# Layer 2 of a four-layer graph network: the low part of the messages made by VectorE straight from PSUM instead of from a second ScalarE copy

## The chip, the core and the metric

The kernel runs on one core of one Trainium2 chip. The metric is the device time of one launch in microseconds (us), taken as the median of three runs: 2426.45 us before the change (2425.6 to 2430.18). The profile is one further execution; its own time is 2429.41 us, and its span, from the first to the last instruction, is 2428.0 us.

## What is computed

Sixteen graphs of 1024 nodes with 256 features go through four layers; each layer is x = x + gnn(relu(layernorm(x))) (layer 3 the same with a four-headed attention). The change is in layer 2:

```python
h = jnp.maximum(_layernorm(x, axis=-1), 0.0)
a = adj.astype(x.dtype)
h2 = jnp.einsum('bnf,fu->bnu', h, W_msg)            # messages
msg_sum = jnp.einsum('bij,biu->bju', a, h2)         # summed over the neighbours i
deg = jnp.sum(a, axis=1)
messages = jnp.where(deg[..., None] > 0, msg_sum / jnp.maximum(deg, 1.0)[..., None], 0.0)
x = x + relu(jnp.einsum('bnf,fu->bnu', h, W_upd) + messages + bias)
```

## The kernel before

**Tiles.** A graph's 1024 nodes are eight tiles of 128 rows (NT = 8), its 256 features two chunks of 128 (DC = 2). `xs` holds a graph's x; `ht` is the normalised, transposed x that feeds the projections. The transposes (`flip`, line 930, by TensorE into `pt_h`) and the copies into `ht` (line 931, ScalarE) are made four at a time.

**Layer 2, first part: projections (lines 1153 to 1160).** For each of the eight node tiles n, `project` (line 936) multiplies `ht` by W_msg into a PSUM tile `ps_proj`. It is full float32, so each of its two matmuls is two passes of TensorE: four matmul instructions in the trace for one n. All projections of all layers share the two buffers of the pool `mm_ps` (tag "mm"); the projection two places later needs the buffer back. The message is then split in two parts that TensorE can multiply in its faster one-pass form F32R: ScalarE writes `hi` = ps_proj times z, rounded to F32R (line 1156), writes the same product again, unrounded, into a float32 tile `rest` in SBUF (line 1158; two buffers, tag "e", which other layers' `e` tiles share), and VectorE writes `lo` = `rest` minus `hi` (line 1159). So `ps_proj` is free again when ScalarE has done line 1158.

**Layer 2, second part: neighbour sums (lines 1161 to 1182).** For each of eight output tiles j, into one PSUM bank `ps_o2` (two buffers): two chunks of the W_upd product (line 1164), then eight F32R matmuls with `hi` and eight with `lo` (line 1170), whose stationary operand is the adjacency `adj_n[j]`, brought in by GpSimd's DMA queue (line 828). ScalarE takes the result out (lines 1178, 1179), VectorE adds the bias and the residual (lines 1180, 1006).

**The order.** Nothing runs in the order in which it is written. Graphs are laid out some 130 us apart in a list of due times, so that the layers of one graph stand beside layers of the next, and then the class `Order` plays the whole program against a table of costs per instruction and writes a fixed order for each engine. At each moment it gives an engine the ready instruction that is earliest in the list. A changed instruction can therefore move its neighbours on every engine. Once built, each engine's queue is strictly in order: an instruction that waits holds up all that stand behind it.

**Beside the projections of layer 2** in the same stretch stand the last projections of layer 0 of the next graph (line 936 with 258 columns, copied out by ScalarE, line 1022), and the last transposes of layer 2's own input, whose scales VectorE makes (lines 901, 902) and ScalarE applies (line 911, `hn`). Lines 986 and 991 are two short VectorE instructions of layer 0, line 953 and the DMAs 955 and 961 make layer 0's row of weights. Layer 3 (line 1225 on VectorE, line 1238 on TensorE with 64-column halves), layer 1 (lines 1109 and 1102) and layer 0 (lines 1048, 1050, 1040) are not touched.

Of the kernel before, what the change touches and what calls it, by code (L numbers as in the profile page):

```python
# [9 lines left out]
F32 = mybir.dt.float32  # L10
U8 = mybir.dt.uint8
AF = mybir.ActivationFunctionType
OP = mybir.AluOpType
AX = mybir.AxisListType

P = 128
# [630 lines left out]
def tile_simple_stack(  # L647
# [11 lines left out]
    nc = tc.nc  # L659
    B, N, D = x.shape  # L660
# [23 lines left out]
    def tile_of(pool, shape, dtype, tag, name, bufs):  # L684
        t = pool.tile(shape, dtype, tag=tag, name=name, bufs=bufs)
        slots[t.tensor.tag] = bufs
        return t
# [11 lines left out]
    work = ctx.enter_context(tc.tile_pool(name="work", bufs=2))  # L699
# [123 lines left out]
    def load_adj(b, g):  # L823

        t = tile_of(state, [P, NT, EIGHTH], F32R, tag="adj", name="adj", bufs=4)
        if b == 0 and g < 4:
            behind(t[:1, 0, :1])
        nc.gpsimd.dma_start(t, adj[b, :, g * EIGHTH : (g + 1) * EIGHTH].rearrange("(i p) c -> p i c", p=P))  # L828
        return t
# [103 lines left out]
    def project(norm, w, n, width):  # L933
        ps = tile_of(mm_ps, [P, HALF], F32, tag="mm", name="ps_proj", bufs=2)
        for c in range(DC):
            nc.tensor.matmul(ps[:, :width], norm.ht[:, c, n * P : (n + 1) * P], w[:, c, :width], start=(c == 0), stop=(c == DC - 1))  # L936
        return ps
# [58 lines left out]
    def residual(xs, i, v, after, e=None):  # L996

        x = xs[:, i, :]
        if i % 2 == 0:
            if i == NT - 2:  # L1000
                after.settle()
            after.flip()
            after.sums = tile_of(small, [P, 2], F32, tag="sums", name="sums", bufs=4)
        if e is not None:
            nc.vector.scalar_tensor_tensor(x, e, 1.0, x, op0=OP.min, op1=OP.add)
        nc.vector.scalar_tensor_tensor(x, v, 0.0, x, op0=OP.max, op1=OP.add, accum_out=after.sums[:, i % 2 : i % 2 + 1])  # L1006
        if i % 2:
            after.pair(xs, i // 2, after.sums)
# [130 lines left out]
    def layer2(b, xs, norm, after):  # L1139

        adj_n = [load_adj(b, g) for g in range(4)]
        z = tile_of(small, [P, NT], F32, tag="z2", name="z2", bufs=2)
        nc.vector.reciprocal(z, norm.times)
        hi = tile_of(state, [P, NT, W3], F32R, tag="hs", name="hi", bufs=3)
        lo = tile_of(state, [P, NT, W3], F32R, tag="hs", name="lo", bufs=3)
        nc.vector.memset(hi[:, :, D : D + 1].bitcast(F32), 1.0)  # L1150
        nc.vector.memset(hi[:, :, D + 1 : D + 2].bitcast(F32), 0.0)
        nc.vector.memset(lo[:, :, D : D + 2].bitcast(F32), 0.0)
        for n in range(NT):
            ps = project(norm, wx[2], n, D)
            by = z[:, n : n + 1]
            nc.scalar.activation(hi[:, n, :D], ps[:, :D], AF.Copy, scale=by)  # L1156
            rest = tile_of(work, [P, D], F32, tag="e", name="rest", bufs=2)
            nc.scalar.activation(rest, ps[:, :D], AF.Copy, scale=by)
            nc.vector.tensor_tensor(lo[:, n, :D], rest, hi[:, n, :D].bitcast(F32), op=OP.subtract)
            yield 0.91  # L1160
        for j in range(NT):
            ps = tile_of(hd_ps, [P, HALF], F32, tag="hd", name="ps_o2", bufs=2)
            for c in range(DC):
                nc.tensor.matmul(  # L1164
                    ps[:, :D], norm.ht[:, c, j * P : (j + 1) * P], wx[2][:, c, D:], start=(c == 0), stop=False,
                    skip_group_check=True,
                )
            for h in (hi, lo):
                for i in range(NT):
                    nc.tensor.matmul(  # L1170
                        ps[:, : D + 2], adj_n[j][:, i, :], h[:, i, : D + 2],
                        start=False, stop=(h is lo and i == NT - 1), skip_group_check=True,
                    )
            k = b * NT + j
            if j + 4 < NE:
                adj_n.append(load_adj(b, j + 4))
            v = tile_of(work, [P, D], F32, tag="v", name="v", bufs=2)
            nc.scalar.activation(v, ps[:, :D], AF.Copy, scale=z[:, j : j + 1])
            nc.scalar.copy(edges[:, k : k + 1], ps[:, D : D + 1])
            nc.vector.tensor_tensor(v, v, rows["bias2"], op=OP.add)  # L1180
            residual(xs, j, v, after)
            yield 1.61
# [120 lines left out]
    def graph(b):  # L1303
        xs = loaded.pop(b)
        m = masks.pop(b)
        norm = Norm()
        if b == 0:
            norm.first = tile_of(small, [P, NT], F32, tag="q", name="first", bufs=4)
        for g in range(NT // 2):
            norm.pair(xs, g)  # L1310
            m.step()
            yield 2.74
        for layer, inputs in ((layer0, (m,)), (layer1, (m.bytes,)), (layer2, ())):
            yield 1.81
            norm.settle()
            norm.flip()
            after = Norm(degrees(b) if layer is layer1 else None)
            yield from layer(b, xs, *inputs, norm, after)
            norm = after
        yield 1.19  # L1320
        norm.flip()
        res = tile_of(state, [P, NT, H, HW], F32, tag="res", name="res", bufs=1)
        hs = yield from layer3(b, xs, m.bytes, norm, res)
        return tail(b, xs, hs, res)
# [51 lines left out]
    ps = tile_of(tr_ps, [P, P], F32, tag="tr", name="ps_bad", bufs=2)  # L1376
# [65 lines left out]
```

## Time and profile before

| | us |
|---|---|
| median of three runs | 2426.45 (2425.6 to 2430.18) |
| the profiled execution, its own time | 2429.41 |
| its span | 2428.0 |
| TensorE (PE) busy | 2361.5, 97% of the span |
| TensorE weight loads (PEld) busy | 2106.7 |
| VectorE (DVE) busy | 1964.4, 81% |
| ScalarE (ACT) busy | 1455.2, 60% |
| GpSimd (POOL) busy | 469.3 |
| mean granted TensorE clock | 0.991 |

A group of instructions is shown with its line, engine, operation, the tiles that it writes and reads, shapes, count, busy time, mean duration, and the idle time of its engine just before it with what ended that. A matmul's duration in the trace is longer than its share of the pipeline, since several are under way at once; so a TensorE that is "busy" can still lose time, and the time from the start of one matmul to the start of the next says more than the busy time does. The chain of work that ended last goes back from the last instruction, at each step to what released it.

The three instructions of the change are groups of 128 (16 graphs by 8 tiles): line 1156 on ScalarE, 60.1 us, 470 ns each; line 1158 on ScalarE, 59.0 us, 473 ns each; line 1159 on VectorE, 53.7 us, 425 ns each.

### The profile page before, as it was taken

The numbers are of one execution on the slowest core, as the hardware profiler recorded it, in microseconds if no ns is written. First come the engines' busy times: TensorE is split into PE (matmuls) and PEld (weight loads), VectorE is DVE, ScalarE is ACT, GpSimd is POOL, SyncE is SP. The second block draws the span as 40 slices with busy tenths as digits, with TensorE's granted clock in tenths as the row PEclk, the third lists the DMA queues.
The fourth block names the chain that finished last, engine by engine and source line by source line (L and its number), as shares of the span: only waits on it lengthen the run. The fifth ranks groups of instructions, "written<-read, shape, count | busy, mean of one in ns | idle before, by whom it ended". The sixth has DMA issues, their size and how long they took to land.

```text
span 2428.0 us, 63180 instructions
## 1 busy us (share of the span) xinstructions
PE 2361.5 (97%) x26244; PEld 2106.7 (87%) x26244; DVE 1964.4 (81%) x3871; ACT 1455.2 (60%) x4062; POOL 469.3 (19%) x454
## 2 busy tenths in 40 slices
PE   7999999999999999999999999999999999999984
PEld 5889888988888889888998989889888998989874
DVE  6478697996979888787897969879787896978867
ACT  5765657567475665757567475665757566475340
POOL 1120310303113031220303113031220303103021
PEclk9999999999999999999999999999999999999997
DMA  5452342624344263342624334263342634244021
GB/s 177 88 110 89 70 97 87 140 85 92 94 105 101 84 126 98 79 97 78 142 93 92 93 101 106 84 119 101 84 97 75 144 93 92 89 104 89 19 63 37
DMA packets 212008, 231.65 MB, mean 95 GB/s; under 512 B 10328, under 2 KB 160960, under 8 KB 211712
## 3 DMA queue, kind: packets, MB, share of 16 engines
q0 software_dynamic: 137728, 83.90, 19.5%
q1 hardware_dynamic: 73984, 143.62, 18.9%
q8 instruction: 208, 3.41, 0.6%
q14 instruction: 88, 0.72, 0.1%
HBM read 210.25 MB, written 17.22 MB: 94 GB/s over the span
## 4 chain that ended last, share of the span: by engine, by line
PE 86%; DMA 5%; ACT 4%; DVE 3%; POOL 1%; issue 1%; SPq 0%; ACTq 0%; DVEq 0%
PE ps_o L1238 18%; PE ps_o L1040 17%; PE ps_proj L936 17%; PE ps_o L1102 16%; PE ps_o L1170 10%; PE ps_o L1164 4%; PE pt_h L930 4%; DMA raw<-in_adj_t 4%; ACT mask L820 1%; DVE p L1225 1%; POOL rs L836 1%; ACT hn L911 1%; ACT hi L1156 1%; DMA d_row<-e_row 0%; DMA row<-d_row 0%
## 5 line engine op out<-in xcount | busy, mean ns | idle before, releaser
L1225 DVE SCALAR_TENSOR_TENSOR p<-row,q,mask 128x1024 f32<-128x1024 f32 x512 | 617.9, 1279 | 63.0 <-PE ps_o L1238 58.6
L936 PE MATMUL ps_proj<-wx,ht 128*128 128x258 f32 (+2 forms) x2048 | 514.3, 387 | 6.7 <-ACT hs L1194 3.9
L1238 PEld LDWEIGHTS ps_o<-hb,p 128*64 128x64 f32 x16384 | 488.1, 138 | 27.8 <-issue 20.6
L1238 PE MATMUL ps_o<-hb,p 128*64 128x65 f32 x16384 | 502.2, 223 | 4.7 <-DVE p L1225 2.3
L1040 PE MATMUL ps_o<-hs,p 128*128 128x256 f32 x2048 | 477.8, 381 | 4.3 <-ACT hs L1052 4.3
L1102 PE MATMUL ps_o<-hs,p 128*128 128x257 f32 x2048 | 468.8, 382 | 3.9 <-ACT v L1127 2.2
L1102 PEld LDWEIGHTS ps_o<-hs,p 128*128 128x128 f32 x2048 | 381.5, 190 | 61.4 <-ACT v L1127 6.9
L936 PEld LDWEIGHTS ps_proj<-wx,ht 128*128 128x128 f32 x2048 | 371.7, 191 | 67.6 <-ACT hs L1082 6.5
L1040 PEld LDWEIGHTS ps_o<-hs,p 128*128 128x128 f32 x2048 | 381.1, 191 | 54.8 <-ACT hs L1052 4.7
L835 POOL TENSOR_SCALAR rs<-mv 128x4 f32<-128x4 f32 (+1 forms) x112 | 44.9, 401 | 1317.6 <-ACT unread L884 1298.9
L836 POOL TENSOR_TENSOR rs<-rs,neg_half 128x4 f32<-128x4 f32 (+2 forms) x144 | 265.9, 1846 | 12.0
L911 ACT ACTIVATE hn<-xs,shift 128x256 f32<-128x256 f32 x384 | 177.1, 504 | 77.3 <-PE pt_h L930 43.0
L1170 PE MATMUL ps_o<-hi,adj 128*128 128x258 f32 x1024 | 202.3, 320 | 2.1 <-ACT hi L1156 1.0
L1246 ACT ACTIVATE res<-ps_o 128x260 f32<-128x260 f32 x128 | 49.8, 389 | 254.2 <-PE ps_o L1238 253.9
L820 ACT ACTIVATE mask<-raw 128x512 uint8<-128x512 int32 x248 | 156.1, 632 | 53.6 <-DMA raw<-in_adj_t 52.7
L930 PE MATMUL pt_h<-ident,hn 128*128 128x128 f32 x1024 | 175.8, 278 | 2.0 <-ACT hn L911 1.8
L1006 DVE SCALAR_TENSOR_TENSOR xs<-v,xs 128x256 f32<-128x256 f32 x384 | 160.3, 418 | 17.8 <-ACT v L1127 11.2
L828 POOL DMA_DIRECT2D adj<-in_adj x128 | 114.8, 899 | 293.9 <-PE ps_o L1170 292.3
L1170 PEld LDWEIGHTS ps_o<-hi,adj 128*128 128x128 f32 x1024 | 150.1, 190 | 14.9 <-ACT hi L1156 5.4
L1048 DVE SCALAR_TENSOR_TENSOR p<-row,q 128x1024 f32<-128x1024 f32 x128 | 161.4, 1271 | 1.8 <-ACT row L980 1.6
L930 PEld LDWEIGHTS pt_h<-ident,hn 128*128 128x128 f32 x1024 | 126.0, 141 | 36.5 <-ACT hn L911 10.3
L931 ACT COPY ht<-pt_h 128x512 f32<-128x512 f32 x256 | 147.1, 575 | 16.8 <-PE pt_h L930 14.0
(124 smaller groups left out, 3009.0 us busy)
## 6 DMA issues: line engine op xcount, KB each, us to landing
raw<-in_adj_t SPq DMA_DIRECT2D x256, 256.0 KB
adj<-in_adj POOLq DMA_DIRECT2D x128, 512.0 KB, 5.3
row<-d_row SPq DMA_DIRECT2D x108, 512.0 KB
xs<-in_x POOLq DMA_DIRECT2D x32, 512.0 KB, 4.4
out<-xs SPq DMA_DIRECT2D x32, 512.0 KB
wx<-in_w SPq DMA_DIRECT2D x3, 256.0 KB
d_row<-e_row SPq DMA_DIRECT2D x45, 4.0 KB
wts<-in_w_t SPq DMA_DIRECT2D x2, 256.0 KB
```

The lines of the kernel that those rows point to most:

```text
L820: nc.scalar.activation(to, raw, AF.Square, accum_out=total)
L836: nc.gpsimd.tensor_tensor(rs[:, :n], rs[:, :n], neg_half[:, :n], op=OP.pow)
L911: nc.scalar.activation(hn, xs[:, 2 * g + k, :], AF.Relu, scale=scale, bias=bias)
L930: nc.tensor.transpose(pt[:, c, k * P : (k + 1) * P], hn[:, c * P : (c + 1) * P], ident)
L936: nc.tensor.matmul(ps[:, :width], norm.ht[:, c, n * P : (n + 1) * P], w[:, c, :width], start=(c == 0), stop=(c == DC - 1))
L1006: nc.vector.scalar_tensor_tensor(x, v, 0.0, x, op0=OP.max, op1=OP.add, accum_out=after.sums[:, i % 2 : i % 2 + 1])
L1040: nc.tensor.matmul(ps[:, :D], ps_[j][:, i * P : (i + 1) * P], hs[:, j, :D], start=(j == 0), stop=(j == NT - 1))
L1048: nc.vector.scalar_tensor_tensor(p, row_a, q[:, j : j + 1], row_b, op0=OP.mult, op1=OP.max)
L1102: nc.tensor.matmul(ps[:, : D + 1], ps_[j][:, i * P : (i + 1) * P], hs[:, j, : D + 1], start=(j == 0), stop=(j == NT - 1))
L1170: nc.tensor.matmul(ps[:, : D + 2], adj_n[j][:, i, :], h[:, i, : D + 2], start=False, stop=(h is lo and i == NT - 1), skip_group_check=True,)
L1225: nc.vector.scalar_tensor_tensor(p, row, q[:, jj, h : h + 1], mask[:, jj, :], op0=OP.max, op1=OP.mult)
L1238: nc.tensor.matmul(pss[g][part, k * HW : (k + 1) * HW], ps_[t][:, i * P : (i + 1) * P][:, part], hbv[:, j + t, h, :], start=(j == 0 and t ...
```

## The change

One pass on VectorE takes the place of one on ScalarE and one on VectorE. `lo` is now ps_proj times z minus `hi`, read from PSUM by VectorE; the tile `rest` is gone. The buffer `ps_proj` is now free when VectorE has done this pass.

```diff
             ps = project(norm, wx[2], n, D)
             by = z[:, n : n + 1]
             nc.scalar.activation(hi[:, n, :D], ps[:, :D], AF.Copy, scale=by)
-            rest = tile_of(work, [P, D], F32, tag="e", name="rest", bufs=2)
-            nc.scalar.activation(rest, ps[:, :D], AF.Copy, scale=by)
-            nc.vector.tensor_tensor(lo[:, n, :D], rest, hi[:, n, :D].bitcast(F32), op=OP.subtract)
+            nc.vector.scalar_tensor_tensor(
+                lo[:, n, :D], ps[:, :D], by, hi[:, n, :D].bitcast(F32), op0=OP.mult, op1=OP.subtract
+            )
             yield 0.91
```

The new instruction is line 1157 of the changed kernel.

## The prediction

> **What bounds the kernel now.** I read the page first: the busy times, then the chain of work that ended last.
>
> ```profile
> PE 2361.5 (97%) x26244; PEld 2106.7 (87%) x26244; DVE 1964.4 (81%) x3871; ACT 1455.2 (60%) x4062; POOL 469.3 (19%) x454
> ...
> PE 86%; DMA 5%; ACT 4%; DVE 3%; POOL 1%; issue 1%; SPq 0%; ACTq 0%; DVEq 0%
> ```
>
> TensorE carries the time. ScalarE has 40% idle over the span, so the 59.0 us that line 1158 costs it are not a gain by themselves. What counts is whether ScalarE or VectorE hold TensorE up in the stretch where the change acts. So I asked for the busy time of that stretch in one graph (from its first message projection at 996.3 us to its first matmul with `lo` at 1009.0); the columns are length, then PE, PEld, DVE, ACT and POOL busy, granted clock, DMA share, GB/s.
>
> ```profile
> 996.30:1009.00 12.70, 12.61 (x68) 10.57 (x67) 3.40 (x11) 11.33 (x31) 1.20 (x2) 1.00 0.17 46
> ```
>
> Here ScalarE is the fuller engine, 11.33 of 12.70 us, and VectorE is idle for 9.3. PE's 12.61 hides waits, since matmuls overlap. The chain in order of time shows them (start, length, what):
>
> ```profile
> 994.31 1.74 PE ps_proj L936 x8
> ...
> 1006.38 0.97 PE ps_proj L936 x4
> 1007.35 0.02 issue
> 1007.37 0.47 ACT hi L1156
> 1007.85 0.37 ACT rest L1158
> 1008.21 0.02 issue
> 1008.23 0.48 ACT hi L1156
> 1008.72 0.04 issue
> 1008.76 2.43 PE ps_o L1170 x18
> ...
> 1015.32 1.91 PE ps_o L1170 x16
> ```
>
> It leaves TensorE for the last two tiles: `hi`, `rest`, `hi`. It also gives TensorE's undisturbed prices: 1.74/8 = 0.217 us for an instruction of a projection (line 1164 likewise), 1.91/16 = 0.120 for an F32R matmul. With these the timeline of TensorE can be audited, from the start of one group to the start of the next:
>
> ```profile
> 1003.09 0.60 PE L1164 MATMUL ps_o<-wx,ht 128*128 128x256 f32 x2
> 1003.33 0.95 PE L1170 MATMUL ps_o<-hi,adj 128*128 128x258 f32 x5
> 1004.14 1.99 PE L936 MATMUL ps_proj<-wx,ht 128*128 128x256 f32 x8
> 1005.84 0.54 PE L1170 MATMUL ps_o<-hi,adj 128*128 128x258 f32 x2
> 1006.21 1.98 PE L936 MATMUL ps_proj<-wx,ht 128*128 128x256 f32 x8
> 1007.85 1.30 PE L1170 MATMUL ps_o<-hi,adj 128*128 128x258 f32 x5
> 1008.99 1.13 PE L1170 MATMUL ps_o<-lo,adj 128*128 128x258 f32 x8
> ```
>
> (A first F32R matmul after float32 ones is recorded some 0.19 us early and its successor late; a pair of groups taken together is right.) From 1003.09 to 1004.14: 1.05 us for 2 x 0.217 + 5 x 0.120 = 1.03. To 1006.21: 2.07 for 8 x 0.217 + 2 x 0.120 = 1.97, so 0.10 lost. To 1008.99: 2.78 for 8 x 0.217 + 5 x 0.120 = 2.33, so 0.45 lost. In all 5.90 us for 5.33 of work: 0.57 lost, all of it on ScalarE. The first loss is the projection of tile 4 and that of tile 6, each waiting for a `rest` (each restarts some 0.1 late after a wait). The second is mostly the last `hi`: the last projection ends at 1008.20, `hi` takes 0.48 more, and TensorE has only four matmuls to put under it. Note that the `rest` in the chain (until 1008.21) ended just when the projection did: taking it away alone would not bring the last `hi` forward. By start times, the same stage is 12.66 us long in twelve of the sixteen graphs (the third to twelfth, fourteenth and fifteenth).
>
> **The change, part by part.**
>
> Removed: 128 instructions of line 1158 at 473 ns on ScalarE, eight per graph, about 3 us of its 11.33 in the stage. Beside TensorE except for the waits above.
>
> Swapped: line 1159 (SBUF, 425 ns) for a scalar-tensor-tensor pass that reads PSUM. The row nearest to it:
>
> ```profile
> L1006 DVE SCALAR_TENSOR_TENSOR xs<-v,xs 128x256 f32<-128x256 f32 x384 | 160.3, 418 | 17.8 <-ACT v L1127 11.2 <-ACT v L1072 2.2
> ```
>
> The same operation on 256 float32 from SBUF takes 418 ns. PSUM against SBUF on VectorE shows only in one-column reciprocals: line 1123 from PSUM 166 ns, line 1051 from SBUF 156. By the rows, 0.43. [...] I take 0.44, and 0.42 to 0.69 as its bounds. The new pass also takes its scalar from memory, one per partition; line 1048, which does, takes 1271 ns for 1024 elements, line 1050, which does not, 1215, so that is 55 ns at most and lies within the bounds.
>
> Moved: the fixed orders change, since `Order` sees ScalarE free earlier. I compared the orders of the two programs as built. The same twelve graphs agree again. There TensorE's order, from the two W_upd matmuls at 1003.09, becomes: projections of tiles 4 and 5 (8 instructions), 4 `hi` matmuls, projections of 6 and 7 (8), 7 `hi` matmuls, the last `hi`, then `lo`. Before it was 5 `hi`, 8, 2, 8, 4, 1. So three more matmuls lie under the last `hi`. DVE moves one `lo` ahead of lines 901 and 902; elsewhere in these graphs only a matmul or two shift, and ScalarE's and VectorE's orders stay. No DMA, SP or POOL instruction changes place.
>
> New wait: projection n+2 needs `ps_proj` back from VectorE, where it had waited for ScalarE. Behind the waiting VectorE pass stand only other `lo` passes and four short ones (0.16 to 0.17 us each). The long passes of other layers come after.
>
> Working it through, with these lags from single instructions of the trace: projection's end to `hi` 0.04, `hi` to VectorE 0.03, either to TensorE 0.05, and a projection ends 0.38 after its last start. TensorE from 1003.09 (+0.03, because lines 901 and 902, on which `hn` waits, now stand behind a `lo`): tile 4 starts at 1003.55, tile 5 at 1004.42, four `hi` at 1005.28, tile 6 at 1005.76, tile 7 at 1006.63, `hi` from 1007.49, the last at 1008.33, first `lo` at 1008.45. Does each wait hold? Tile 4 ends at 1004.58, its `hi` at 1005.10, its `lo` at 1005.57, the buffer is free for TensorE at 1005.62, wanted at 1005.76: 0.14 to spare. Tile 7's buffer: 0.14 to spare likewise. The last `hi`: tile 7 ends at 1007.66, `hi` at 1008.18, at TensorE 1008.23, wanted at 1008.33: 0.10 to spare. The last `lo` is ready about 1008.7, wanted 0.84 after the first, at 1009.3. So all of the 0.57 goes, less 0.03: 0.54 per graph. [...]
>
> Sum: 12 x 0.54 = 6.5 us. The other four by the same counting: graphs 1 and 2 had two matmuls under the last `hi` and get four, 2 x 0.12 = 0.24 each; graph 13 had two and gets seven, some 0.6; graph 16 loses only the waits on `rest`, 0.1. That is 1.2, in all 7.7. What is late next in the stage is nothing but TensorE's own work. I carry the gain to the end in full: every chain from before the stage to after it runs through these projections, VectorE is idle in it for 9.3 of 12.7 us, and the DMA pieces of the chain (5%) start from work that comes after the stage and shift with it. Against the profiled execution: 2429.41 - 7.7 = 2421.7. The median of the runs is 2.96 below that execution, so 2426.45 - 7.7 = 2418.7.
>
> **The rivals.**
>
> *Given back downstream (little or no change).* For it: layer 3 keeps VectorE at back-to-back passes of line 1225 for stretches (1279 ns each), and GpSimd's adjacency loads and the mask's loads pace some of the chain. Against: they are released by TensorE's progress. If half or more is lost, 2422 to 2427; middle 2424.
>
> *PSUM buffers held by VectorE (slower).* Place: projections of tiles 6 and 7. Two buffers turn over in 1.03 (projection) + 0.04 + 0.48 + 0.03 + L + 0.05 = 1.63 + L, L being the length of a `lo`, while TensorE has 8 x 0.217 + 4 x 0.120 = 2.21 of work. From L = 0.58 it waits; each of two turns costs L - 0.58 + 0.1. They eat the 0.54 at L = 0.75, and at L = 0.9 cost 0.3 a graph net, about 5 us: 2431. [...] Against: the 418 ns row.
>
> *The change does nothing to the bound.* The last `hi` would wait as before, were the order not moved; then only the waits on `rest` go, 0.1 x 16: 2424.8. The built order speaks against it.
>
> **How the numbers follow.** A difference of 0.2% (4.9 us) is about what a measurement can tell from none: faster is below 2421.6, slower above 2431.3. The forecast: 0.62, from 2414 to 2421.6 but for 0.05 below that. Little or no change by either of the two rivals: 0.25, most of it above 2421.6, a little (0.03) below. Slower by the held buffers: 0.13, 2431 to 2440. So faster 0.65, same 0.22, slower 0.13. TensorE's whole loss in these sixteen stages, by start times, is 14.7 us, which no gain should pass; 2414 to 2428 leaves out the slower case and that 0.05.
>
> **What would show it.** In the new profile: line 1156's `hi` no longer followed by 1158; line 1157 near 0.44 us; the stage from first projection to first `lo` 12.1 us instead of 12.66; no wait of line 936 for line 1157; the chain without ScalarE before the last `hi`. Wrong would be: a line 1157 over 0.6 us, line 936 waiting for it, or a stage that is shorter while the distance from graph to graph stays.

## The result, and the profile after

The changed kernel took 2422.64 us in the median of 22 runs (2418.47 to 2426.15), beside 2425.77 for the kernel before (22 runs): ratio 0.9985 [0.9979, 0.9991], 3.1 us less. The time lies within the range of 2414 to 2428, but the gain of 7.7 us isn't there, and 0.15% is under the 0.2% from which the forecast spoke of a faster kernel. Three later comparisons of the same kernel, given below, came to 0.9976, 0.9975 and 0.998; weighted by their intervals the four make 0.9981, some 4.6 us. All four intervals lie below 1, so there is a gain, about half of the forecast.

The profiled execution took 2423.97 us, its span 2422.2, at a clock of 0.991. Its busy times and its chain by engine:

```profile
PE 2357.7 (97%) x26244; PEld 2105.2 (87%) x26244; DVE 1971.6 (81%) x3871; ACT 1410.8 (58%) x3934; POOL 468.7 (19%) x454
...
PE 87%; DMA 4%; DVE 3%; ACT 3%; issue 1%; POOL 1%; SPq 0%; DVEq 0%; ACTq 0%; POOLq 0%
```

ScalarE lost 128 instructions and 44 us of busy time, VectorE gained 7. The two lines of the change in the table of groups (busy us, mean ns, idle time before them and its releaser):

```profile
L1156 ACT ACTIVATE hi<-ps_proj,z 128x256 fp32r<-128x256 f32 x128 | 60.2, 470 | 39.4 <-PE ps_proj L936 39.3
L1157 DVE SCALAR_TENSOR_TENSOR lo<-ps_proj,z,hi 128x256 fp32r<-128x256 f32 x128 | 61.7, 484 | 100.6 <-ACT hi L1156 100.5
```

And from the view of line 1157 alone, who waited for it (us, times):

```profile
  PEld ps_proj L936: 1.4, 8
```

The pass takes 484 ns, and TensorE's projections wait for it 8 times in the whole span, 1.4 us together (only the weight load ahead of the matmul waits). All 8 lie in the first, second, thirteenth and sixteenth graph (2, 2, 3 and 1), none in the twelve like ones. TensorE's timeline in the same stretch of a like graph as was shown of before:

```profile
997.01 0.60 PE L1164 MATMUL ps_o<-wx,ht 128*128 128x256 f32 x2
997.44 1.89 PE L936 MATMUL ps_proj<-wx,ht 128*128 128x256 f32 x8
998.98 0.82 PE L1170 MATMUL ps_o<-hi,adj 128*128 128x258 f32 x4
999.64 1.91 PE L936 MATMUL ps_proj<-wx,ht 128*128 128x256 f32 x8
1001.20 1.32 PE L1170 MATMUL ps_o<-hi,adj 128*128 128x258 f32 x8
1002.35 1.12 PE L1170 MATMUL ps_o<-lo,adj 128*128 128x258 f32 x8
```

From the W_upd matmuls to the first `lo` it is 1002.35 - 997.01 = 5.34 us for 5.33 of work, where it had been 5.90: TensorE no longer waits. The chain says the same. It runs through the stretch on TensorE alone, with the projections, four `hi` and the rest in one row, and no ScalarE before the last `hi`:

```profile
997.60 1.73 PE ps_proj L936 x8
999.33 0.47 PE ps_o L1170 x4
999.80 1.74 PE ps_proj L936 x8
1001.55 3.01 PE ps_o L1170 x25
```

So the stretch that the prediction was about came out as forecast, and the question is where more than 3 us went. I measured in each trace, by single matmul starts, the stage (first message projection to first `lo` matmul) of every graph, and the distance from each stage's end to the start of the next graph's stage. One distance stands out, the one from the thirteenth stage to the fourteenth. In us, with the kernels of the experiments:

| kernel | 1st, 2nd | twelve like ones, each | 13th | 16th | all 16 | 13th to 14th |
|---|---|---|---|---|---|---|
| before | 13.20 | 12.66 | 13.51 | 12.99 | 204.83 | 133.05 |
| changed | 13.06 | 12.16 | 12.46 | 13.35 | 197.83 | 135.54 |
| e1_twelve | 13.21 | 12.17 | 13.54 | 13.00 | 198.97 | 132.64 |
| e2_four | 13.07 | 12.67 | 12.47 | 13.35 | 204.20 | 136.20 |
| e3_not_thirteenth | 13.05 | 12.15 | 13.52 | 13.33 | 198.81 | 132.85 |
| e4_new_ops_old_order | 13.07 | 12.68 | 13.27 | 13.18 | 204.76 | 132.70 |
| e5_old_ops_new_order | 13.80 | 12.51 | 13.13 | 13.37 | 204.18 | 136.47 |
| e6_lo_twice | 15.18 | 13.92 | 13.89 | 14.93 | 226.27 | 136.05 |
| e7_changed_again | 13.06 | 12.16 | 12.45 | 13.34 | 197.82 | 135.95 |
| e8_spliced | 13.06 | 12.16 | 12.45 | 13.34 | 197.81 | 133.56 |
| e9_changed_third | 13.06 | 12.16 | 12.44 | 13.33 | 197.77 | 136.31 |
| e10_spliced_again | 13.06 | 12.16 | 12.44 | 13.34 | 197.82 | 133.32 |
| e11_changed_fourth | 13.06 | 12.16 | 12.45 | 13.34 | 197.82 | 135.80 |

The like stages of one kernel agree to 0.02 us (but for one of 12.82 in e2_four). The other distances move by 1 us or so from one execution to the next whatever the kernel (up to 2.5 now and then, once 3.7), and so does the end, so the sum of all distances can't be used for differences of a few us.

### The profile page after: what moved, and what is told of

Its sections match the earlier page's. It is cut to its first block, busy times and chain, and to the rows that moved or that the text cites. A ratio compares the mean times of both kernels' runs of the same rounds, so it can differ in the third digit from the quotient of the medians.

```text
span 2422.2 us, 63061 instructions
## 1 busy us (share of the span) xinstructions
PE 2357.7 (97%) x26244; PEld 2105.2 (87%) x26244; DVE 1971.6 (81%) x3871; ACT 1410.8 (58%) x3934; POOL 468.7 (19%) x454
## 4 chain that ended last, share of the span: by engine, by line
PE 87%; DMA 4%; DVE 3%; ACT 3%; issue 1%; POOL 1%; SPq 0%; DVEq 0%; ACTq 0%; POOLq 0%
PE ps_o L1238 17%; PE ps_proj L936 17%; PE ps_o L1040 17%; PE ps_o L1102 16%; PE ps_o L1170 10%; PE ps_o L1164 4%; PE pt_h L930 4%; DMA raw<-in_adj_t 3%; DVE p L1225 1%; POOL rs L836 1%; ACT mask L820 1%; DMA d_row<-e_row 1%; ACT hn L911 0%; DVE p L1109 0%; DMA row<-d_row 0%
## 5 line engine op out<-in xcount | busy, mean ns | idle before, releaser
L1225 DVE SCALAR_TENSOR_TENSOR p<-row,q,mask 128x1024 f32<-128x1024 f32 x512 | 617.8, 1279 | 63.0 <-PE ps_o L1238 60.1
L1170 PE MATMUL ps_o<-hi,adj 128*128 128x258 f32 x1024 | 193.4, 316 | 0.3
L1109 DVE SCALAR_TENSOR_TENSOR p<-row,q,mask 128x1024 f32<-128x1024 f32 x128 | 155.8, 1271 | 2.1 <-ACT row L980 1.2
```

The lines of the kernel that those rows point to most:

```text
L1170: nc.tensor.matmul(ps[:, : D + 2], adj_n[j][:, i, :], h[:, i, : D + 2], start=False, stop=(h is lo and i == NT - 1), skip_group_check=True,)
L1225: nc.vector.scalar_tensor_tensor(p, row, q[:, jj, h : h + 1], mask[:, jj, :], op0=OP.max, op1=OP.mult)
```

## Where it went: the thirteenth graph

The chain of the changed kernel behind the thirteenth graph's stage, in order of time:

```profile
1901.19 2.25 PE ps_proj L936 x10
...
1906.26 0.70 POOL rs L835
...
1907.04 1.90 POOL rs L836
...
1908.96 0.49 ACT hs L1194
...
1909.49 2.06 PE ps_proj L936 x8
...
1912.92 2.43 PE ps_o L1040 x10
```

And the kernel before, at the same place of its program:

```profile
1909.07 2.68 PE ps_proj L936 x12
1911.75 0.86 PE ps_o L1040 x4
...
1913.05 1.78 PE ps_proj L936 x8
```

Before, the chain never leaves TensorE: the projections of layer 3 (line 936 with 264 columns, taken out of PSUM by ScalarE in line 1194) stand between groups of line 1040. In the changed order the chain leaves TensorE for GpSimd. The projection of the seventh node tile needs the PSUM buffer of the fifth back from line 1194, and line 1194 needs for the fifth a scale that GpSimd still has to make (lines 835 and 836). The waits of this stretch name it (total us, times, longest us):

```profile
ACT hs L1194 <- POOL rs L836: 1.6, 1, 1.6
...
PE ps_proj L936 <- ACT hs L1194: 1.2, 1, 1.2
...
PE ps_o L1040 <- ACT v L1072: 0.5, 1, 0.5
```

TensorE's own two waits are 1.7 of the 3.1 us by which this distance is longer (mean of the four executions of the changed kernel 135.90; of before, e1_twelve, e3_not_thirteenth and e4_new_ops_old_order 132.81). By start times they cost, with TensorE's restarts, 1.4 + 0.7 = 2.1; the rest I haven't itemised.

TensorE does not get to that projection sooner than before. Counted from the end of the thirteenth stage (1884.46 us before, 1876.05 in the changed kernel), it would have started it at 32.06 us without the wait, against 31.97 before. What is late is the scale: line 836 ends at 32.88 instead of 31.05, 1.83 us later. Of that, 0.82 arises ahead of GpSimd, where VectorE and ScalarE take the first tiles of layer 3 ahead of some work for the statistics of its last ones (line 879 starts 1.1 us later), and 1.0 in GpSimd's own two instructions. The same pair before:

```profile
1913.85 0.21 POOL L835 TENSOR_SCALAR rs<-mv 128x4 f32<-128x4 f32 x1 [1.86 <-ACT unread L884]
1914.14 1.36 POOL L836 TENSOR_TENSOR rs<-rs,neg_half 128x4 f32<-128x4 f32 x1
```

They took 0.21 + 1.36 = 1.57 us here, and 0.70 + 1.90 = 2.60 in the changed order. This repeats in every trace: about 1.57 where the old order stands there, about 2.58 where the new one does. Beside them VectorE runs other instructions in the two orders: lines 1204 and 1203 before, 1292, 1050 and 1203 in the changed kernel.

## The experiments

All times below are medians, each beside runs of the kernel before on the same chip.

**e1_twelve: the change in the twelve like graphs only.**

```diff
+            if b not in (0, 1, 12, 15):
                 nc.vector.scalar_tensor_tensor(
...
+            else:
+                rest = tile_of(work, [P, D], F32, tag="e", name="rest", bufs=2)
```

> The new low part in twelve graphs only (the third to twelfth, the fourteenth and the fifteenth, whose order around layer 2 is the same); the first, second, thirteenth and sixteenth keep the two ScalarE copies and with them the old order. Theory 'four graphs': each of the twelve shortens its stage by 0.50 us, nothing downstream takes that back, and what is missing from the forecast is lost by the new order of the other four: 6.0 us faster than before (ratio 0.9975), faster than the full change by some 3. Rival 'swallowed downstream': every graph loses half of its half microsecond later: 2 to 3 us faster (0.999), no faster than the full change. Stage length 12.16 us in the twelve under both.

Measured: 2423.87 against 2429.75, ratio 0.9977 [0.997, 0.9985]. The twelve stages lose 12 x 0.49 = 5.9 us and the time falls by 5.9 (by the interval 3.6 to 7.3). As far as this can be measured the gain of these graphs arrives in full; that half of it is swallowed on the way does not fit.

**e2_four: the change in the other four only.**

```diff
+            if b in (0, 1, 12, 15):
```

> The complement: the new low part in the first, second, thirteenth and sixteenth graph only. Theory 'four graphs': their stages get 1 us shorter in sum, but TensorE waits some 1.2 us for line 1194 (layer 3's projections, now ahead of the GpSimd power of line 836) and 0.5 for line 1072 after the thirteenth graph: 1 to 3 us slower than before (1.0004 to 1.0012). Rival 'swallowed downstream': 0 to 1 us faster. In the profile: a wait of line 936 for line 1194 of about 1.2 us near 1915 us under the first theory, in any run with this order.

Measured: 2431.63 against 2429.75, ratio 1.0008 [0.9999, 1.0016]. Their stages got shorter by 0.6 us, and the kernel became no faster; the distance behind the thirteenth is 136.20. By the table one expects -0.6 + 3.1 = +2.5, and +1.9 came out. The interval just includes no difference.

**e3_not_thirteenth: the change everywhere but in the thirteenth.**

```diff
+            if b != 12:
```

> The new low part in fifteen graphs, the thirteenth keeps the old form and the old order. Theory 'four graphs': the thirteenth is the main loser (stage 1.05 shorter, 2.3 lost after it), so this is 1.2 us faster than the full change, 4 to 5.5 us faster than before (0.998). Rival 'swallowed downstream': 15/16 of what the full change gains, about 2.9 us (0.9988).

Measured: 2423.54, ratio 0.9973 [0.9963, 0.9984]. The thirteenth stage is as long as before (13.52), and the distance behind it also (132.85). The stages save 6.0 us, the time fell by 6.2. So leaving out the graph for which I had forecast the largest single gain costs nothing that can be measured.

**e4_new_ops_old_order: the new instructions in the order of before.** Each engine's planned order is changed, by a list, into the one that it had before the change.

```diff
+        for e, changes in MOVES.items():
+            for i1, i2, new in reversed(changes):
+                order[e][i1:i2] = new
```

> The new instructions in the old order: a list of moves after the planner puts TensorE, VectorE and ScalarE in the order of the kernel before (without line 1158). Theory 'order': the last hi still has four matmuls above it and waits 0.25 plus a restart of 0.1; only the two waits for rest can go, 0.19 us a graph: stage 12.47 to 12.6 us in the twelve, 1 to 3 us faster than before. Rival 'ScalarE's relief': the stage shortens to 12.2 with the old order too, and the run is 5 us faster or more, since the losing order after the thirteenth graph is gone as well.

Measured: 2429.61 against 2429.75, ratio 1.0002 [0.9993, 1.001]; I had expected 1 to 3 us less. The like stage is 12.68 us, nothing gained. Two waits in its trace say why (lines are 10 higher in this kernel):

```profile
PEld ps_proj L946 <- DVE lo L1167: 0.4, 2, 0.2
...
PEld ps_o L1180 <- ACT hi L1166: 0.3, 1, 0.3
```

The waits on `rest` are gone, but waits on `lo` have come in their place. The buffer turns over in 1.63 + 0.48 = 2.11 us, and the old order gives TensorE only two projections and two `hi` matmuls meanwhile, 8 x 0.217 + 2 x 0.120 = 1.98. That is the small part, 0.13. The last `hi` is waited for as before, and by start times this loses the same 0.45 us.

**e5_old_ops_new_order: the old instructions in the new order**, with line 1158 right behind each line 1156. The code that puts the list in is that of e4_new_ops_old_order.

> The old instructions (two ScalarE copies, VectorE subtracts) in the new order: moves after the planner put every engine in the order of the changed kernel, with line 1158 right behind its line 1156. Theory 'order': seven hi matmuls lie under the last hi, the wait is gone without any relief of ScalarE: stage 12.2 to 12.3 us in the twelve, and the same time as the full change, 2 to 5 us faster than before. Rival 'ScalarE's relief': hi comes late behind rest, stage 12.6 us or longer, no gain or slower, since the loss after the thirteenth graph stays.

Measured: 2429.2 against 2429.52, ratio 1.0001 [0.9993, 1.0009]. The like stage is 12.51 us: the last `hi` has its cover, but the second pass on ScalarE now holds up something else, the transposes of layer 2's own input:

```profile
PEld pt_h L940 <- ACT hn L921: 1.0, 3, 0.5
```

The first two graphs even become 0.6 us longer. So neither half of the change gives the 0.5 us per graph (the new order alone 0.15, the new instructions alone nothing); it takes ScalarE's relief and the new order together.

**e6_lo_twice: every `lo` written twice**, with the orders of the changed kernel.

```diff
             nc.vector.scalar_tensor_tensor(
                 lo[:, n, :D], ps[:, :D], by, hi[:, n, :D].bitcast(F32), op0=OP.mult, op1=OP.subtract
             )
+            nc.vector.scalar_tensor_tensor(
+                lo[:, n, :D], ps[:, :D], by, hi[:, n, :D].bitcast(F32), op0=OP.mult, op1=OP.subtract
+            )
```

> The changed kernel with every low part written twice in a row by VectorE, all orders as in the changed kernel: the length of a low part goes from 0.48 to some 0.86 us. By the forecast's turnover of two buffers, 1.63 + 0.86 = 2.49 against 2.21 of TensorE's work: 0.28 and a restart of 0.1 on each of two turns, 0.76 us a graph: stage 12.9 us in the twelve, 12 us slower than the full change, 8 to 9 slower than before. If VectorE's queue and not the buffers sets the price, or later work hides it, less than 3 us slower than before.

Measured: 2453.42 against 2429.52, ratio 1.0096 [1.0081, 1.0112], and 30.5 us more than the changed kernel beside it. The like stage grew by 1.76 us, more than twice what the formula gives. Three things were too small in it. The second pass follows the first only 0.52 us after its start, so that `lo` takes 0.52 + 0.48 = 1.0 us. There are more turns of the buffers than two. And lines 901 and 902, which stand behind the passes on VectorE, make `hn` late, so that the transposes wait too. Two rows of TensorE's timeline (lines 11 higher, in brackets the idle time before and its releaser):

```profile
1007.10 0.93 PE L941 MATMUL pt_h<-ident,hn 128*128 128x128 f32 x4 [0.20 <-ACT hn L922]
...
1013.54 2.05 PE L947 MATMUL ps_proj<-wx,ht 128*128 128x256 f32 x8 [0.21 <-DVE lo L1171]
```

What it also shows: the stages together are 28.4 us longer than in the changed kernel, and 30.5 arrive at the end. Stage time lost is paid for in full here.

**e7_changed_again: the changed kernel beside these.**

> The changed kernel once more, on this chip and with a second profile. If the wait for line 1194 after the thirteenth graph comes from the fixed order, it is there again, 1.2 us within 0.3, and the stages are 12.16 us again; if it was chance in the first profile, it is gone. Time 2 to 5 us below before.

Measured: 2422.93 against 2429.52, ratio 0.9976 [0.9966, 0.9987]. The distance behind the thirteenth stage is 135.95 again, with the same wait of 1.2 us, so it belongs to the order and not to one execution.

**e8_spliced: the changed kernel, but between the thirteenth and the fourteenth stage every engine in its order of before.** The code is that of e4_new_ops_old_order, with a list that covers this stretch alone.

> The changed kernel's instructions and orders everywhere, but between the thirteenth and the fourteenth message stage every engine follows the order that it had there before the change (24 places on TensorE, 25 on VectorE, 18 on ScalarE; nothing else moves). My theory, that 3.2 us of the 7.0 saved in the stages are given back there because layer 3's projections were moved ahead of layer 2's and wait for a GpSimd power: the stages sum to 197.8 us as in the changed kernel, the distance from the thirteenth stage to the fourteenth is 133.0 us instead of 135.5 to 136.5, and the time is 7 us below before, ratio 0.9971 (changed kernel: 0.9985 and 0.9976). Rival, that the stage of the thirteenth graph hands its gain to whatever comes next, so that the distance grows whichever order follows: 135 to 136 us, ratio 0.9983.

Measured: 2423.18 (9 runs) against 2428.96, ratio 0.9972 [0.9962, 0.9982].

**e9_changed_third: the changed kernel on the same chip.**

> The changed kernel once more, for the comparison on the same chip. My theory: 3.8 us below before, ratio 0.9984, distance after the thirteenth stage 135.5 to 136.5 us, 3 us slower than the kernel with the order put back. Rival: equal to that kernel within 0.05%.

Measured: 2423.56 (8 runs), ratio 0.9975 [0.9965, 0.9986]. The distance behind the thirteenth stage is 133.56 with the order put back and 136.31 without, so the rival that it grows whichever order follows has fallen. GpSimd's pair is back at 0.21 + 1.36 us. In the spliced kernel's chain TensorE is again alone (lines 10 higher):

```profile
1904.24 2.68 PE ps_proj L946 x12
```

The list puts back the order of TensorE, VectorE and ScalarE together, so it doesn't tell which of the three made the scale late.

But the times of the two kernels hardly differ, where I had expected 3 us. A comparison of this size couldn't tell the two apart, so both ran again.

**e10_spliced_again and e11_changed_fourth.**

> The kernel with the order put back, a second time, since its first comparison was too coarse for a difference of 3.2 us. My theory, that what is given back after the thirteenth stage arrives at the end of the kernel: with the earlier runs pooled, 3.2 us below the changed kernel (2 to 4.5); distance after the thirteenth stage 133 to 133.6 us. Rival, that the later wait costs its 3 us there but is made up before the end: within 1 us of the changed kernel.

> The changed kernel beside it on the same chip. My theory: 3.8 us below before, and 3.2 us above the kernel with the order put back. Rival: equal to it within 1 us.

Measured: 2420.78 (9 runs), ratio 0.9975 [0.9965, 0.9984], and 2423.02 (12 runs), ratio 0.998 [0.9971, 0.9988], both against 2427.51. The distances are 133.32 and 135.80. The difference of the mean times, spliced against changed, is 0.6 us (95% interval -1.3 to 2.6) in the first pair and 1.7 (0.3 to 3.1) in the second; the two averaged, 1.2 (0.0 to 2.4). My expectation of 3.2 (2 to 4.5) wasn't met, and the rival's "within 1 us" is not met cleanly either. In the traces the order put back wins 135.90 - 133.44 = 2.5 us where it acts (0.6 of the 3.1 remain), and no later distance gives it away again in a way that stands out from their scatter. At the end of the kernel somewhere between nothing and 2.4 of it is seen.

## Why the prediction was right in its stretch and missed in the sum

**The cost of the pass.** Forecast 0.44 us, bounds 0.42 to 0.69; measured 0.484 (477 to 486 in all 128). No row or run shows a pass of 256 elements at the 0.69 of the upper bound: the longest of line 1157 took 0.486. Line 1157 is 484 - 418 = 66 ns over line 1006, and differs from it in two things, the PSUM source and the scalar per partition. By this kernel's own rows the scalar costs some 55 ns (line 1048 with it 1271 ns, line 1050 without 1215; line 1109, which reads the mask as line 1050 does, 1270) and PSUM 10 (the one-column reciprocals, line 1123 from PSUM 166 ns, line 1051 from SBUF 156), 65 together. That is an estimate from passes of 1024 columns and of one; no run here separates the two on 256. I had worked out the 55 and then put them at nothing. The miss has no effect on the twelve graphs, as 0.484 is under the 0.58 from which the prediction's formula lets TensorE wait: what held was a buffer turnover of 2.11 us against 2.21 of work. In the other four the sign "line 936 waiting for it" did come, 8 times, 1.4 us.

**The twelve like graphs.** Forecast 0.54 us each, 6.5 together; measured 0.50, 6.0. The audit of TensorE by single starts was right, and so was the reason given, that the order and the free ScalarE act together: e4_new_ops_old_order and e5_old_ops_new_order, each with one of the two, became no faster by anything that can be measured. The third rival, in which the waits on `rest` alone would bring 0.1 per graph, was too kind: without the order they are replaced by waits on `lo`.

**Held PSUM buffers.** The mechanism is real and not far away. In the twelve like graphs it wasn't at work at 0.484 us; at 1.0 us, in e6_lo_twice, the projections' weight loads wait 1.9 us for `lo` in one like stage (6 times), and the kernel is 23.9 us slower than before, where two turns of 1.0 - 0.58 + 0.1 less the 0.54 would have made 0.5 a graph, 8 us. The formula of this rival left out the other turns and the short VectorE instructions queued behind `lo`.

**The other four graphs: the step that failed.** "The other four by the same counting: ... That is 1.2", and "I carry the gain to the end in full". Their stages did lose 0.28 (first two, 0.48 forecast) and 1.05 (thirteenth, 0.6 forecast), but the sixteenth grew by 0.36 where I had it shrink by 0.1. That is 1.0 in all, near the 1.2. What I had not looked at is what else the plan changed in a graph that does not agree with the others. I compared the orders of these graphs only up to the first `lo`. Behind the thirteenth stage it let VectorE and ScalarE serve layer 3's first tiles ahead of the statistics of the last ones, and put GpSimd's pair beside other VectorE instructions. The scale comes 1.83 us later, TensorE waits for it, and the distance is 3.1 us longer. So "No DMA, SP or POOL instruction changes place" was true and not enough: the two GpSimd instructions kept their places and took 1.0 us more. The longer distance is in all seven traces with the new order there, whatever the instructions, and in none of the six with the old one. The prediction had named the sign itself, a stage that is shorter while the distance from graph to graph stays: it came true in one graph. The statement that VectorE's idle time and the DMA pieces let the gain through holds for the twelve (e1_twelve: 5.9 of 5.9). The argument failed because the gain of the stage and the order behind it come from the same re-planning.

The sum: stages -7.0, the thirteenth distance +3.1, together -3.9 or 0.9984. Measured were 0.9985, 0.9976, 0.9975 and 0.998. The rival "given back downstream" had the right size, 2422 to 2427, and the wrong place: not the passes of line 1225 nor DMA, and not in every graph, but once. That the time still fell into 2414 to 2428 is no merit of the argument, since the range was drawn to hold this rival too.

**What stays open.** How much of the 3.1 us reaches the end: e8_spliced to e11_changed_fourth say 0.0 to 2.4 of the 2.5 us that the old order wins back in the trace, so a part may be made up later, in waits that scatter too much to be read. e5_old_ops_new_order points the same way: by the table its stages (-0.65) and this distance (136.47 - 132.81 = 3.66) make it 3.0 us slower than before, and it was no slower (at most 2.2 by the interval). Why the planner went wrong there is only argued: its table gives lines 835 and 836 on four columns 286 and 450 + 4 x 160 = 1090 ns, together 1.38 us whatever stands beside them, and the new order made 2.60 of it where the old one had made 1.57. A corrected table wasn't tried. That VectorE's instructions beside it slow GpSimd is read from where they stand in the traces (1.57 us beside lines 1204 and 1203, 2.60 beside 1292, 1050 and 1203); no run moved them alone. Why the sixteenth stage grew wasn't followed up either; with the old order (e4_new_ops_old_order) it is 13.18, about half way.

The lowest ratios against before are those of e8_spliced and e3_not_thirteenth (0.9972, with 0.9975 the second time, and 0.9973). Against the changed kernel, which came to 0.9975 to 0.9985, their lead is at the edge of what was measured.

## What to carry to other kernels

When a planner writes the order, an edit has two effects, its own and that of the new order, and they are to be audited apart: in the stage where the instructions are, and wherever the built orders first differ and last differ. Graphs that agree can be costed once and multiplied; the one that does not agree deserves the longest look, above all behind the stage in question. When a PSUM buffer's last reader changes engine, compare the turnover with the work that the order puts in it before counting any gain: here 2.11 us against 2.21 in the new order, so no wait, and against 1.98 in the old one, where new waits took the place of those removed. Then look at the last result that TensorE waits for: how much work lies over it was worth 0.45 of the 0.5 us a graph.

## What was not expected of the hardware

Line 836 on GpSimd takes 1242 ns in the mean on four columns of the changed kernel, but no single one takes that. In the trace of before 65 of its 96 instructions took 1.01 to 1.06 us, among them those beside a pass of line 1159 or 1225; 13 took 1.36, beside lines 1204, 1203 and 1295; and 17 took 1.90 to 1.96, most of them beside lines 1048, 1180 and 1050. The trace doesn't tell why. Two passes of VectorE, of which the second overwrites what the first wrote, start 0.52 us apart, 0.04 more than one lasts (in e6_lo_twice, 1004.22 and 1004.74), while the next pass, on another tile, starts 0.40 after (1005.14). A VectorE pass of 256 float32 with one source in PSUM and its scalar per partition takes 484 ns, against 418 with both sources in SBUF and a constant for its scalar.
